# A causal mask moved out of the matrix engine's products, and a LoRA stage moved into the attention phase's tiles

## The chip, the core and the metric

The kernel runs on one core of a Trainium2 chip. A core has five engines with queues of their own: TensorE (PE, matrix products; PEld is its weight load), VectorE (DVE), ScalarE (ACT), GpSimd (POOL) and SyncE (SP, which here issues all DMAs). The metric is the device time of one execution in microseconds; lower is better. A profiled execution gives a page and a trace. L1391 means line 1391 of the kernel before.

## What is computed

Sixteen sequences of 512 tokens with 256 channels pass through six residual stages: a gated feed-forward with 4-bit block quantisation, a Mamba scan, the feed-forward again, a mixture of LoRA experts, causal attention with ALiBi, and the same mixture again. Each starts with a layer norm. The last three are what the change touches:

```python
x = x + 0.5 * lora(layernorm(x))
x = x + attn(layernorm(x))
x = x + 0.5 * lora(layernorm(x))

def lora(x):                            # 8 experts of rank 8
    result = x @ base_w.T + base_b
    gating = softmax(x @ router_w.T + router_b).astype(bfloat16)
    mid = x @ lora_A
    return result + 2 * einsum('bsr,erd,bse->bsd', mid, lora_B, gating)

def attn(x):                            # 16 heads of 16 channels
    q, k, v = heads(x @ Wq + bq), heads(x @ Wk + bk), heads(x @ Wv + bv)
    scores = q @ k.T / 4 - slope[h] * abs(kpos - qpos)
    scores = where(kpos > qpos, -inf, scores)
    return (softmax(scores) @ v) @ Wo + bo
```

## The kernel before

All sixteen sequences ("batches", b = 0 to 15) stay in SBUF as `xs[b]`, 128 partitions x 4 token blocks x 256. A framework (Tile) lays tiles into pools, puts in the waits, and orders each engine's instructions by priorities of its own, except where the kernel holds them to program order (`keep_in_program_order`): `matmul` (L1199) and `transpose` (L1202) of the attention phase do. A tile name with n buffers can be written for the (n+1)-th time only when its first use is done with.

**First LoRA stage**, `lora_phase` (L947), in pools of its own ("l" in SBUF; in PSUM two pools with the tags `ob`, `tr`, `o`, two buffers each, all eight banks). A software pipeline over b: `norm(b)` (statistics on DVE, a Sqrt on ACT, the reciprocal on DVE, four scalings on ACT), `turn(b-1)` (eight transposes, two copies on ACT), `base(b-2)` (sixteen matmul instructions as the trace counts them, with router and LoRA-A columns beside the 256; additions on DVE; a softmax over eight experts, whose Exp is on ACT) and `experts(b-3)` (transposes, a copy, eight matmuls, two additions). Sqrt and Exp are in different ACT tables, and each change costs an ACT_TABLE_LOAD. Between its steps the stage calls the generator `constants(aw)` (L1102), which loads attention's weights and fills its constant tiles. Behind the last batches it norms and turns batch 0 again (L1071 to L1080) and projects it to queries, keys and values by `heads` (L1251), with value tiles as spare room.

**Attention**, `attn_phase` (L1084). After the LoRA pools are closed, pools "a" (SBUF), `ps_s` (PSUM: `sp` two buffers and `sw` one, two banks each) and `ps` (tag `mm`, two single banks) are opened, the ACT table for Exp and Ln is loaded (L1467), and `begin(1)` (L1471) starts batch 1's norm. A unit is a batch and a group j of four heads; 64 units are pipelined over three turns of the main loop. In turn u there are six steps (three parts of the triangle x two pairs of heads). Each step has for unit A = u the peak scores (`peak_score`, products of 32 rows) and their maxima (`peak_max`: DVE adds a causal mask, then reduces); for unit C = u - 1 (or, in step 0, for Dn = u - 2) the same scores the other way round with the maximum taken off (`weigh_score`), and the exponential into `eT` (`weigh_exp`). Step 0 also has `peak_rows` (transposes of the maxima `mx`, and `qm`, queries with the maximum in a row) and `apply`, the weighted sums of Dn's values with `eT`. `aside` (L1483) fills each step with pieces of the next batch's projections (`project`, L1205), divisions and output projections.

A head takes 32 rows of `qs` and `ks`: 16 channels, row RS = 16 for the ALiBi term, row RM = 17 for the maximum; the other 14 are zero. Eight DMAs on SP per `q` or `k` half bring the 16 channel rows of each head to their places (L1288).

The causal mask of the exponentials is on PE: `weigh_exp` adds -1e30 in PSUM with two products of a bf16 identity `id16` and `mask_k`, 128 columns wide in parts 0 and 1, 256 in part 2, before ACT's Exp reads the bank.

**Last LoRA stage** (L1515 to L1692): the same computation in attention's pools as generators (`mix_norm`, `mix_turn`, `mix_base`, `mix_experts`). `mix_norm` has Ln and Exp on ACT, and two Newton steps and two more operations on POOL, ten of 4 elements. `mix_rest` orders them in rounds. Its working tiles (`parts`, L1519) are the `q`/`k` tiles of batch 14, free by then, and one `eT` tile. Two batches (`mix_first`) run beside attention's last batch, the other fourteen mostly behind it.

Of the kernel before, what the change touches and what calls it, by code (L numbers as in the profile page):

```python
# [36 lines left out]
def macaron_kernel(  # L37
# [83 lines left out]
    def transpose_seq(xh, dst, psum_pool, tag, order=lambda ins: ins):  # L121

        for k in range(KD):
            pt = psum_pool.tile([P, SEQ], F32, name="pt", tag=tag)
            for c in range(NC4):
                order(nc.tensor.transpose(  # L126
                    pt[:, c * P : (c + 1) * P], xh[:, c, k * P : (k + 1) * P], ident
                ))
            nc.scalar.copy(dst[:, k, :], pt)

# [50 lines left out]
    def ffn_phase(weights, src, dst, prepare=None, raws=(), keep=()):  # L181
        wgT, wuT, wdT = weights
        HF = DFF // 2
        with tc.tile_pool(name="f", bufs=2) as fp, tc.tile_pool(
# [90 lines left out]
            def make_h(b, pair, j):  # L275
# [3 lines left out]
                for half in range(2):  # L279
# [11 lines left out]
                    nc.scalar.activation(sl, g, AF.Silu)  # L291
# [655 lines left out]
    def lora_phase(weights, last, beside=None, heads=None):  # L947


        wx, lb, br = weights  # L950
        W = D + NE + NR
        with tc.tile_pool(name="l", bufs=2) as lp, tc.tile_pool(
            name="l_b", bufs=2, space=PSUM
        ) as ps_b, tc.tile_pool(name="l_ps", bufs=2, space=PSUM) as ps:
            xhs, xTs, copies = {}, {}, []

            cbs = []
            for i in range(3):
                cb = lp.tile([P, NC4, NX], F32, name=f"cb{i}", tag=f"cb{i}", bufs=1)
                nc.gpsimd.memset(cb[:, :, NE * NR :], 1.0)  # L960
                cbs.append(cb)

            def norm(b):

                x = xs[b]
                st = lp.tile([P, NC4, 6], F32, name="st", tag="st")
                mv = lp.tile([P, NC4, 2], F32, name="mv", tag="mv")
                for c in range(NC4):
                    nc.vector.bn_stats(out=st[:, c, :], in_=x[:, c, :])
                    nc.vector.bn_aggr(out=mv[:, c, :], in_=st[:, c, :])  # L970
                sd = lp.tile([P, NC4], F32, name="sd", tag="sd")
                nc.scalar.activation(sd, mv[:, :, 1], AF.Sqrt, bias=eps)
                rs = lp.tile([P, NC4], F32, name="rs", tag="rs")
                nc.vector.reciprocal(rs, sd)
                nm = lp.tile([P, NC4], F32, name="nm", tag="nm")
                nc.vector.scalar_tensor_tensor(
                    nm, mv[:, :, 0], -1.0, rs, op0=ALU.mult, op1=ALU.mult
                )
                xh = lp.tile([P, NC4, D], F32, name="xh", tag="xh")
                for c in range(NC4):  # L980
                    nc.scalar.activation(
                        xh[:, c, :], x[:, c, :], AF.Identity,
                        bias=nm[:, c : c + 1], scale=rs[:, c : c + 1],
                    )
                xhs[b] = xh

            def turn(b):
                xT = lp.tile([P, KD, SEQ], F32, name="xT", tag="xT")
                transpose_seq(xhs.pop(b), xT, ps, "tr")
                xTs[b] = xT  # L990

            def base(b):

                xT = xTs.pop(b)
                s = lp.tile([P, NC4, NE + NR], F32, name="s", tag="s")
                for half in range(2):
                    o = ps_b.tile([P, 2, SEQ], F32, name="ob", tag="ob")
                    for j in range(2):
                        c = 2 * half + j
                        for k in range(KD):  # L1000
                            nc.tensor.matmul(  # L1001
                                o[:, j, :W], lhsT=xT[:, k, c * P : (c + 1) * P],
                                rhs=wx[:, k, :], start=(k == 0), stop=(k == KD - 1),
                            )
                    nc.vector.tensor_tensor(
                        s[:, 2 * half : 2 * half + 2, :], o[:, :, D:W],
                        br.unsqueeze(1).to_broadcast([P, 2, NE + NR]), op=ALU.add,
                    )
                    xc = xs[b][:, 2 * half : 2 * half + 2, :]
                    nc.vector.tensor_tensor(xc, xc, o[:, :, :D], op=ALU.add)  # L1010
                lg, mid = s[:, :, :NE], s[:, :, NE:]
                mx = lp.tile([P, NC4], F32, name="mx", tag="mx")
                nc.vector.tensor_reduce(mx, lg, axis=AX.X, op=ALU.max)
                ex = lp.tile([P, NC4, NE], F32, name="ex", tag="ex")
                nc.vector.tensor_tensor(
                    ex, lg, mx.unsqueeze(2).to_broadcast([P, NC4, NE]), op=ALU.subtract
                )
                nc.scalar.activation(ex, ex, AF.Exp)
                nc.vector.tensor_reduce(mx, ex, axis=AX.X, op=ALU.add)
                nc.vector.reciprocal(mx, mx)  # L1020
                gt = lp.tile([P, NC4, NE], BF16, name="gt", tag="gt")
                nc.vector.tensor_tensor(
                    gt, ex, mx.unsqueeze(2).to_broadcast([P, NC4, NE]), op=ALU.mult
                )
                cb = cbs[b % 3]
                nc.vector.tensor_tensor(
                    cb[:, :, : NE * NR].rearrange("p c (e r) -> p c e r", e=NE),
                    gt.unsqueeze(3).to_broadcast([P, NC4, NE, NR]),
                    mid.unsqueeze(2).to_broadcast([P, NC4, NE, NR]), op=ALU.mult,
                )  # L1030

            def experts(b):
                cb = cbs[b % 3]
                pt = ps.tile([P, SEQ], F32, name="ct", tag="tr")
                for c in range(NC4):
                    nc.tensor.transpose(
                        pt[:NX, c * P : (c + 1) * P], cb[:, c, :], ident
                    )
                cT = lp.tile([NX, SEQ], F32, name="cT", tag="cT")
                copies.append(nc.scalar.copy(cT, pt[:NX, :]))  # L1040
                for half in range(2):
                    o = ps.tile([P, 2, D], F32, name="o", tag="o")
                    for j in range(2):
                        c = 2 * half + j
                        nc.tensor.matmul(  # L1045
                            o[:, j, :], lhsT=cT[:, c * P : (c + 1) * P], rhs=lb,
                            start=True, stop=True,
                        )
                    xc = xs[b][:, 2 * half : 2 * half + 2, :]
                    nc.vector.tensor_tensor(xc, xc, o, op=ALU.add)  # L1050
                if last:
                    store_x(b)

            for b in range(NB + 3):
                if 0 <= b - 3:
                    experts(b - 3)
                if 0 <= b - 2 < NB:
                    base(b - 2)
                if 0 <= b - 1 < NB:
                    turn(b - 1)  # L1060
                if b < NB:
                    norm(b)
                if heads is not None:
                    if 0 < b < NB:
                        next(beside, None)
                        if b % 2:
                            next(beside, None)
                    if b == NB - 1:
                        for _ in beside:
                            pass  # L1070
                    if b == NB:  # L1071
                        norm(0)
                    if b == NB + 1:
                        turn(0)
                        first = heads(0, xTs.pop(0), None, ps, "tr", nc.tensor.matmul)
                        for _ in range(4):
                            next(first)
                    if b == NB + 2:
                        for _ in first:
                            pass  # L1080
        return copies[-1]


    def attn_phase(weights):  # L1084
# [4 lines left out]

        RS, RM = HD, HD + 1  # L1090
        NJ = NH // 4
# [10 lines left out]
        def constants(aw):  # L1102
# [46 lines left out]
            for i in range(2):  # L1149
                for j in range(NJ):  # L1150
                    q = aw.tile([P, SEQ], F32, name=f"q{i}{j}")
                    nc.vector.tensor_scalar(
                        q, pos, 0.0, is_s, op0=ALU.mult, op1=ALU.add
                    )
                    qs.append(q)
                    k = aw.tile([P, SEQ], F32, name=f"k{i}{j}")
                    nc.vector.tensor_scalar(
                        k, pos, slope[:, j : j + 1], neg_m, op0=ALU.mult, op1=ALU.add
# [36 lines left out]
        def at(b, j):  # L1195
            return (b % 2) * NJ + j

# [665 lines left out]
```

## Time and profile before

| | us |
|---|---|
| three runs | 4329.03, 4329.45, 4329.85 |
| median | 4329.45 |
| profiled execution | 4323.53 |
| its span, first to last instruction | 4321.8 |

The page gives each engine's busy time over that span:

```profile
PE 3980.8 (92%) x18786; PEld 2179.5 (50%) x18786; DVE 3735.6 (86%) x4950; ACT 2315.4 (54%) x3478; POOL 1672.8 (39%) x1102
```

These are averages over six stages. By the windows of the trace the first feed-forward and the scan last to 2440 us, the second feed-forward to about 2990, the first LoRA stage to 3141, attention to about 4213, and the rest of the last LoRA stage to the end. The costliest groups of the LoRA and attention stages, by the page (line, engine, operation, output<-input, partitions x elements, count | busy us, mean ns of one | idle time of that engine just before, and what ended it):

```profile
L1397 ACT ACTIVATE eT<-s 128x768 f32<-128x768 f32 (+1 forms) x384 | 338.6, 882 | 481.0 <-PE s L1200 481.0
L1200 PE MATMUL s<-k,q 32*128 32x256 f32 (+3 forms) x2048 | 479.5, 477 | 5.4 <-DVE mx L1350 4.5
L1350 DVE TENSOR_REDUCE mx<-s 128x2 f32<-128x1024 f32 (+3 forms) x512 | 410.3, 823 | 12.4
L1200 PE MATMUL s<-qm,k 32*128 32x512 f32 (+3 forms) x2048 | 387.1, 473 | 8.9 <-ACT eT L1397 7.7
```

The matmuls of attention all have line 1200, that of the helper, so they are told apart by their tiles. An fp32 product shows as two matmuls. Products of 32 rows run side by side in the array, so their busy time is not a sum; starts and distances between starts are what to read.

### The profile page before, as it was taken

The page shows a single profiled execution, that of the slowest core. Times are in us where ns is not written, and L with a number is a line of the kernel's source. Part 1 is how long each engine was busy: PE and PEld are TensorE (multiplying, and loading weights), DVE is VectorE, ACT ScalarE, POOL GpSimd, SP SyncE. Part 2 cuts the span into 40 slices and gives each one's busy share as a digit, 9 for nine tenths or more (in the row PEclk, how much of TensorE's full clock was granted, in tenths as well). Part 3 has the DMA queues.
Part 4 walks back from the last instruction along what each step waited for, and adds up shares of the span by engine and source line. Part 5 has one row for each costly group of instructions (what it writes and reads, how often), then busy time and mean ns, then how long its engine had stood idle before and what let it go on. Part 6 is the DMA issues. An engine that isn't in the chain of part 4 may idle for free. (4 is left out here: it accounts for less than half of the span.)

```text
span 4321.8 us, 51496 instructions
## 1 busy us (share of the span) xinstructions
PE 3980.8 (92%) x18786; PEld 2179.5 (50%) x18786; DVE 3735.6 (86%) x4950; ACT 2315.4 (54%) x3478; POOL 1672.8 (39%) x1102
## 2 busy tenths in 40 slices
PE   6999977989888899888888799998999999999999
PEld 4666632333333333333333466666745555555557
DVE  9999838999999999999999899997678778878776
ACT  4444346676767677677666344434624444444434
POOL 3000027888888888888889400000000000000001
PEclk9999999999999999999999999999989999999999
DMA  4000024344444444444442300000010000000002
GB/s 151 15 15 20 15 109 129 119 137 128 127 132 133 141 142 142 142 142 141 142 139 82 114 1 1 1 1 16 2 24 16 18 19 16 18 20 14 20 11 69
DMA packets 120895, 305.16 MB, mean 71 GB/s; under 512 B 25329, under 2 KB 45362, under 8 KB 104002
## 3 DMA queue, kind: packets, MB, share of 16 engines
q1 hardware_dynamic: 120642, 301.88, 22.3%
q8 instruction: 148, 2.42, 0.2%
q14 instruction: 105, 0.86, 0.1%
HBM read 239.68 MB, written 45.35 MB: 66 GB/s over the span
## 5 line engine op out<-in xcount | busy, mean ns | idle before, releaser
L487 POOL TENSOR_TENSOR bx<-dtu,bc 128x1024 f32<-128x1024 f32 x512 | 1193.6, 2359 | 47.5 <-DVE h L883 47.3
L493 PE MATMUL y<-g,ident 128*128 128x512 f32 x2048 | 1007.3, 630 | 130.3 <-DVE g L490 130.1
L883 DVE TENSOR_TENSOR_SCAN h<-da,bx 128x1024 f32<-128x1024 f32 x384 | 879.7, 2291 | 85.4 <-ACT da L484 48.8
L484 ACT ACTIVATE da<-dt,a_neg 128x511 f32<-128x511 f32 x1024 | 703.0, 688 | 217.7 <-DVE hs L883 117.6
L493 PEld LDWEIGHTS y<-g,ident 128*128 128x128 f32 x2048 | 388.3, 198 | 710.0 <-issue 461.9
L1397 ACT ACTIVATE eT<-s 128x768 f32<-128x768 f32 (+1 forms) x384 | 338.6, 882 | 481.0 <-PE s L1200 481.0
L490 DVE TENSOR_TENSOR g<-h,bc 128x1024 f32<-128x1024 f32 x384 | 468.9, 1221 | 28.6 <-DVE h L883 1.4
L1200 PE MATMUL s<-k,q 32*128 32x256 f32 (+3 forms) x2048 | 479.5, 477 | 5.4 <-DVE mx L1350 4.5
L1350 DVE TENSOR_REDUCE mx<-s 128x2 f32<-128x1024 f32 (+3 forms) x512 | 410.3, 823 | 12.4
L1200 PE MATMUL s<-qm,k 32*128 32x512 f32 (+3 forms) x2048 | 387.1, 473 | 8.9 <-ACT eT L1397 7.7
L1600 POOL MEMSET k<- 128x4 f32 x2 | 0.2, 105 | 950.4 <-DVE ku L1282 946.9
L1346 DVE TENSOR_TENSOR s<-s,mask 128x256 f32<-128x256 f32 (+1 forms) x384 | 199.3, 519 | 194.1 <-PE s L1200 191.2
L487 POOL TENSOR_TENSOR g<-hs,bc 128x1024 f32<-128x1024 f32 x128 | 301.3, 2354 | 157.7 <-DVE hs L883 140.4
L291 ACT ACTIVATE sl<-g 128x352 f32<-128x352 f32 x256 | 118.1, 464 | 384.6 <-PE g L286 381.6
L1200 PEld LDWEIGHTS s<-k,q 32*128 32x128 f32 x2048 | 218.6, 186 | 164.1 <-DVE s L1346 80.5
L883 DVE TENSOR_TENSOR_SCAN hs<-da,bx 128x1024 f32<-128x1024 f32 x128 | 291.9, 2281 | 2.5 <-ACT da L484 2.5
L493 PE MATMUL p<-xT,w_in 128*128 128x512 f32 x500 | 242.2, 607 | 19.7 <-ACT xT L484 10.1
L484 ACT ACT_TABLE_LOAD x170 | 218.1, 1283 | 3.0
L960 POOL MEMSET cb<- 128x4 f32 x3 | 0.2, 104 | 561.4 <-PE o L331 561.4
L1200 PEld LDWEIGHTS s<-qm,k 32*128 32x128 f32 x2048 | 170.8, 186 | 58.7 <-ACT eT L1397 42.0
L516 POOL MEMSET xs<- 128x12 f32 x2 | 0.2, 110 | 512.7 <-DMA xd<-x 512.7
L286 PE MATMUL g<-wgT,xT 128*128 128x352 f32 x512 | 182.4, 466 | 0.0
(311 smaller groups left out, 6925.6 us busy)
## 6 DMA issues: line engine op xcount, KB each, us to landing
bc<-bd SPq DMA_DIRECT2D x128, 1024.0 KB, 6.6
xs<-xc SPq DMA_DIRECT2D x240, 256.0 KB, 4.7
xc<-xp SPq DMA_DIRECT2D x60, 256.0 KB, 2.0
x<-_attn_hidden_states_dram SPq DMA_DIRECT2D x16, 512.0 KB, 7.6
xd<-x SPq DMA_DIRECT2D x16, 512.0 KB, 2.6
xo<-xd SPq DMA_DIRECT2D x16, 512.0 KB, 3.6
xe<-xo SPq DMA_DIRECT2D x16, 512.0 KB, 2.6
x<-xe SPq DMA_DIRECT2D x16, 512.0 KB, 10.2
```

Of the source, the lines that this page charges most:

```text
L286: nc.tensor.matmul(dst, lhsT=xT[:, k, c * P : (c + 1) * P], rhs=w[:, k, f0 : f0 + HF], start=(k == 0), stop=(k == KD - 1),)
L291: nc.scalar.activation(sl, g, AF.Silu)
L484: return tc.keep_in_program_order(nc.scalar.activation(out, in_, func, **kw))
L487: tc.keep_in_program_order(nc.gpsimd.tensor_tensor(out, in0, in1, op=op))
L490: tc.keep_in_program_order(nc.vector.tensor_tensor(out, in0, in1, op=op))
L493: tc.keep_in_program_order(nc.tensor.matmul(out, **kw))
L516: nc.gpsimd.memset(t[:, :, : DCONV - 1], 0.0)
L883: tc.keep_in_program_order(nc.vector.tensor_tensor_scan(flat(h), flat(das[t % 2]), flat(bxs.pop(t)), 0.0, op0=ALU.mult, op1=ALU.add,))
L1200: tc.keep_in_program_order(nc.tensor.matmul(out, **kw))
L1346: nc.vector.tensor_tensor(own, own, const["mask"][:, :w].unsqueeze(1).to_broadcast([P, 2, w]), op=ALU.add)
L1350: nc.vector.tensor_reduce(mx[:, t, 2 * pair : 2 * pair + 2, RM], s[:, :, off : off + (t + 1) * P], axis=AX.X, op=ALU.max,)
L1397: const["exp"] = nc.scalar.activation(eT[:, 2 * pair : 2 * pair + 2, e0 : e0 + w], s[:, :, :w], AF.Exp)
```

## The change

**The mask of the exponentials.** `id16`, `mask_k` and the products are gone. The zero rows 18 to 29 of a head now stand for the twelve 32-key blocks (four token blocks c, i = 1 to 3): `ks` has a 1 there for the keys of its block, and `mx`, hence `qm`, has -1e30 there for the queries of block c before 32 i. The score product itself so masks every 32-key block that lies wholly ahead of a query. What remains, keys ahead of the query within one block of 32, is set to zero after Exp by an `affine_select` on POOL, in place in `eT`.

```diff
+        BLOCKS = [(c, i, RM + 3 * c + i) for c in range(NC4) for i in range(1, 4)]
...
+            last = ks[-1]
+            nc.vector.tensor_scalar(last, pos, 0.0, neg_m, op0=ALU.mult, op1=ALU.add)
+            for c, i, row in BLOCKS:
+                nc.vector.tensor_scalar(
+                    last[:, P * c + 32 * i : P * c + 32 * i + 32],
+                    prow.to_broadcast([P, 32]), float(row), neg_m,
+                    op0=ALU.is_equal, op1=ALU.add,
+                )
...
-                    nc.vector.tensor_scalar(
-                        k, pos, slope[:, j : j + 1], neg_m, op0=ALU.mult, op1=ALU.add
-                    )
+                    nc.vector.scalar_tensor_tensor(
+                        ks[i * NJ + j], pos, slope[:, j : j + 1], last,
+                        op0=ALU.mult, op1=ALU.add,
+                    )
...
                     nc.gpsimd.memset(mx, 0.0)
+                    for c, i, row in BLOCKS:
+                        nc.gpsimd.memset(mx[: 32 * i, c, :, row : row + 1], MASKED)
...
         def weigh_exp(b, j, part, pair, s, eT):
-            w = len(WEIGH[part]) * P
-            for i in range(2):
-                matmul(
-                    s[:, i, :w], lhsT=const["id16"],
-                    rhs=const["mask_k"].rearrange("p i e -> p (i e)")[:, :w],
-                    start=False, stop=True, skip_group_check=True,
-                )
             w = 512 if part == 0 else 384
             const["exp"] = nc.scalar.activation(
                 eT[:, 2 * pair : 2 * pair + 2, e0 : e0 + w], s[:, :, :w], AF.Exp
             )
+            n = len(WEIGH[part])
+            own = eT[:, 2 * pair : 2 * pair + 2, e0 : e0 + n * P]
+            nc.gpsimd.affine_select(
+                out=own, in_=own, compare_op=ALU.is_ge, fill=0.0, base=0,
+                pattern=[[0, 2], [0, n], [1, P]] if n > 1 else [[0, 2], [1, P]],
+                channel_multiplier=-1,
+            )
```

**The first LoRA stage.** `lora_phase` and `heads` are gone (`heads` is again the body of `project`). Attention's pools are opened straight after the feed-forward. `mix_rest` becomes `mix_rounds(first)`, run once with 0 for the first stage and once with 2 as before for the last. While `free` is empty, that is in the first stage, `parts` works in two `eT` tiles, nothing is stored, and each round also takes a step of `constants`; from round 16 on batch 0's `project` runs between its steps. The ACT table is loaded behind the feed-forward's last Silu. All three value tiles are filled with ones by `constants`.

```diff
-            behind = lora_phase(weights, False, constants(aw), heads)
...
-                with tc.issue_after(behind.ins):
+                with tc.issue_after(silu[-1].ins):
                     const["exp"] = nc.scalar.preload_act_table_set("natural_log_exp_and_others")
...
+                    for n in range(first + 1, NB + 4):
...
+                        if first + 2 <= n < NB:
+                            mix_norm(n)
+                        if not free:
+                            if n < NB:
+                                next(making, None)
+                            if n == NB:
+                                begin(0)
+                                normed = coming.pop(0)
+                            if n == NB + 1:
+                                coming[0] = normed
                         for of in (
                             turn, base, base, expert, turn, base, expert, base, expert
                         ):
...
+                making = constants(aw)
+                for _ in range(2):
+                    rows_of.append(ap.tile([P, 4, EW], F32, name="eT", tag="eT"))
+                mix_norm(0)
+                mix_norm(1)
+                for _ in mix_rounds(0):
+                    next(coming.get(0, none_left), None)
+                for _ in coming.pop(0):
+                    pass
+                started.clear()
+                begin(1)
```

In the built program the instructions of PE, DVE, ACT, POOL and SP stand in the same order in both kernels up to the end of the second feed-forward (but for the table load). From the first `qm` on, ACT's are the same, PE's differ by the 768 mask products and DVE's by a few swaps of small operations.

## The prediction

> **What bounds the kernel now.** I read the page's totals and slices first, then the windows by stage, then the timeline inside the stages that the diff touches. By slices, TensorE (PE) is the engine that is full in the last third of the span, where both LoRA stages and attention lie. The windows divide that third (columns: start and end, length, then PE, PEld, DVE, ACT and POOL busy with instruction counts, granted clock, DMA share, GB/s).
>
> ```profile
> PE   6999977989888899888888799998999999999999
> DVE  9999838999999999999999899997678778878776
> POOL 3000027888888888888889400000000000000001
> 2990.00:3141.00 151.00, 132.66 (x634) 102.84 (x633) 106.58 (x415) 94.49 (x174) 3.78 (x12) 0.97 0.06 15
> 3141.00:3175.00 34.00, 27.58 (x81) 11.06 (x82) 23.76 (x67) 3.99 (x8) 2.11 (x2) 0.60 0.14 31
> 3175.00:4110.00 935.00, 927.28 (x7650) 499.08 (x7649) 739.97 (x1371) 391.19 (x520) 0.10 (x1) 0.99 0.08 18
> ```
>
> Three stages, three limits. The first LoRA stage (2990 to 3141) has PE at 88%, DVE at 71%, ACT at 63%. The first attention unit (3141 to 3175) runs at a granted clock of 0.60. Attention proper has PE busy 99% of 935 us, DVE 79%, POOL nothing: a microsecond taken out of PE's stream there is a microsecond of span, as long as DVE can follow. All earlier stages issue the same instructions in both kernels, and so do ACT and (but for a few small swaps) DVE in attention: they are costed at nothing because nothing of them changes.
>
> **Part 1: the mask products leave PE.** Each of the 384 exponentials (64 units of 4 heads, 6 each) is preceded by two bf16 products of `id16` with `mask_k` (L1391): 128 columns in parts 0 and 1, 256 in part 2. Their busy time overlaps their neighbours', so I take the distance from the first product of a pair to the next other matmul:
>
> ```profile
> 3601.05 0.39 PE L1200 MATMUL s<-mask_k,id 128*128 128x256 bf16 x2
> 3601.37 1.12 PE L1200 MATMUL s<-k,q 32*128 32x512 f32 x2
> ...
> 3607.82 0.28 PE L1200 MATMUL s<-mask_k,id 128*128 128x128 bf16 x2
> 3607.94 0.61 PE L1203 MATMUL p<-ident,oT 128*128 128x128 f32 x4
> ```
>
> 0.12 us for a narrow pair, 0.32 for this wide one (0.23 where a transpose follows). Summed so over the trace: 256 narrow pairs 35.3 us, 128 wide pairs 37.7, together 73.0, or 1.14 per unit. A unit takes 16.05 us (from one `qm` to the next, over a batch: 17.7, 15.3, 15.6, 15.6), so PE alone would bring it to 14.9.
>
> Not all of that is had. DVE is busy 13.4, 13.5, 12.8 and 11.3 us in those four units; the second would have 13.5 in 14.1. And at a quarter of the unit borders the transposes of `mx` already wait 0.35 us for DVE's last maximum, where 0.23 of mask is hidden anyway: 16 x 0.23 = 3.7. I give back 12 us in all, 4 for those borders and 8 (half a microsecond per batch) for the tight unit. Bounds: 0 back, or half of the gain (36) if DVE's order becomes the limit.
>
> **Part 2: GpSimd's selection stands between exp and the weighted sum.** POOL gets 384 selections on fp32, in place: 256 elements a partition (parts 0, 1) or 512 (part 2). Only the last of a unit can be felt: the next PE work after it is that unit's `apply`, whose third block (c = 2) reads what it wrote. The rows:
>
> ```profile
> L1177 POOL TENSOR_SCALAR_AFFINE_SELECT mask_k<-mask_k x2: 292/292/292, 3031.5 to 3031.7; 128x128 bf16<-128x128 bf16 x2
> 3603.40 0.39 PE L1200 MATMUL s<-mask_k,id 128*128 128x256 bf16 x2
> 3603.83 0.81 ACT L1397 ACTIVATE eT<-s 128x768 f32<-128x768 f32 x1 [1.54 <-PE s L1200]
> 3604.45 2.36 PE L1200 MATMUL o<-eT,va 128*32 128x512 f32 x32
> ```
>
> Take M as the moment when the scores end and the mask pair now starts. In most units exp ends at M + 1.24 and c = 2 starts 1.05 later, at M + 2.29. Without the pair PE's c = 2 comes 0.23 earlier, at M + 2.06; exp needs no mask and, with the same distance from last matmul to exp (0.3 us), ends at about M + 0.95. ACT to POOL costs 0.08 (ACT `rs` ending 4201.20, POOL `g` starting 4201.28), POOL to the next about the same. So the selection has some 0.95 us. The trace has it only at 128 elements. Below, a POOL memset of 512 (0.52 us); above, four times 0.292 (1.17; the 1024-element product at 2.36 us gives the same rate). Splitting 0.292 into the 0.104 of a 4-element memset and a rest that grows with the elements, 0.104 + 4 x 0.188 = 0.86: just hidden. I charge 3 us; bounds 0 and 64 x 0.25 = 16. POOL has the room: 4 x 0.48 + 2 x 0.86 = 3.6 us of a 15 us unit, with nothing else queued there but the 10-op norm chains of the last batch.
>
> The Trainium skill ("GPSIMD Engine Reference", 3.1) has about 1.8 cycles per element at 1.2 GHz at best for a one-input loop; 512 elements would be 0.77 us before dispatch, by an estimate from that page, and the charge would be 0. The same skill speaks against the change in "SBUF — State Buffer" (SBUF: two separate sides): a DVE instruction with two SBUF inputs and a reading GpSimd instruction exclude each other for their whole length. The row it bears on is `x<-x,bob` (682 ns, two a batch); if every one of the 32 held up a last selection it would be 32 x 0.68 = 22 us. But the one that stands nearest to a unit's border, at 3601.46, starts 2.3 us before that unit's last exp does, so by this rule only stray ones could count, under 2 us. No run here shows the lock.
>
> **Part 3: the first LoRA stage in the rounds of the last one.** Removed are the Sqrt and Exp table loads, 9 of each at 1.28 us; the norm becomes Ln and Exp on ACT (0.2 us each) and ten 4-element POOL operations, 2.7 us a batch (4201.28 to 4204.02).
>
> ```profile
> 3013.83 0.60 PE L126 MATMUL pt<-ident,xh 128*128 128x128 f32 x4
> ...
> 3118.10 1.04 PE L126 MATMUL pt<-ident,xh 128*128 128x128 f32 x8
> ...
> 4263.69 0.20 ACT L1545 ACTIVATE rs<-v 128x4 f32<-128x4 f32 x1
> ...
> 4270.40 0.21 ACT L1545 ACTIVATE rs<-v 128x4 f32<-128x4 f32 x1
> ```
>
> From the third batch's transposes to the sixteenth's the old stage takes 104.3 us, 8.0 a batch. The last stage, which has the rounds already, repeats every 6.7 with PE never waiting. The first one also carries the statistics (4 x 0.41 + 4 x 0.16 a batch) and the constants on DVE, so I take 7.2: 13 x 0.8 = 10.5 gained; bounds 17 and 0.
>
> Its start: POOL now does five large memsets (2 x 0.52, 3 x 1.06), 24 small ones (0.04 to 0.10 each) and two iotas before the first norm chain, 6 to 7.5 us from 2993.9, then 2.7 of chain. First transposes at 3003 to 3005 instead of 2999.9. DVE's next `mv` waits for POOL there, with base(0)'s additions queued behind it. Batches 2 and 3 share one chain, and I get the third batch's transposes at 3014, as now: 0, within 3 either way.
>
> Its end: after the last transposes there remain 5.8 us of that round, base(15) 3.6, three `mix_experts` at 2.1 (lag 4, not 3) and the projections 11.2, some 27, plus 3 of waits in two shared PSUM banks: 30 against 22.9 now (3118.1 to 3141.0). 7 lost; bounds 4 and 12. The stage: 4 gained, from 13 gained to 12 lost. The 32 q/k row DMAs (0.62 us each on SP) are the same ones in the same order, and begin before the last three expert steps as now.
>
> **Part 4: the first unit.** Norm 1 now uses a pool that opened long before:
>
> ```profile
> 3148.55 2.30 PE L1203 MATMUL p<-ident,xh 128*128 128x128 f32 x8 [6.42 <-DVE xh L1235]
> 3157.94 1.65 PE L1200 MATMUL s<-k,q 32*128 32x256 f32 x8
> ```
>
> Today PE starts at 3141.0, idles 6.4 us because `xh` of batch 1 was begun only then, and runs on at half clock; the first `qm` comes at 3168.3, 27.3 us later. In the new order that `xh` stands on DVE before the last softmaxes of the LoRA stage. Then the unit is DVE's six additions and maxima, 2 x 1.65 + 2 x 1.38 + 2 x 1.72 = 9.5, plus 2.5 for first score, transposes and waits: 12. Gain 15; bounds 16 and, if the clock falls again, 3.
>
> **Sum.** -73 + 12 + 3 - 15 - 4 = -77. The span of 4321.8 becomes 4245, its execution (1.7 more) 4246.5. The three runs' median, 4329.45, is 5.9 above the profiled execution; on it I put the same difference: 4252.
>
> **The rivals.** (a) DVE becomes the bound in attention and half of part 1 is lost: -36 + 3 - 15 - 4 = -52, 4277. For it: 13.5 us of 14.1 in the tight unit. Against: 51 us of 59.6 over a batch, two score buffers. (b) The LoRA stage comes out 12 longer (POOL's memsets first, two PSUM banks) and PE is cold again in unit 0: -73 + 12 + 3 - 3 + 12 = -49, 4280. For it: the queue order above; against: the last stage's 6.7. (c) Slower: the selection itself. It costs 64 times what it exceeds 0.95 us by, and eats the remaining 80 at 0.95 + 80/64 = 2.2 us for 512 elements, 4.3 ns each, nearly twice the 2.3 of any row. At 3 us: 64 x 2.05 = 131, 4380. (d) No change: the pairs were hidden by drains of the array that stay; then parts 1 and 2 give nothing and part 3 loses what part 4 wins, 4329. Against: PE's next work follows each pair at once.
>
> **How the numbers follow.** Forecast 0.70 (4232 to 4270), (a) 0.14, (b) 0.08, (c) 0.05, (d) 0.03. A change of 0.2%, some 9 us, is about what can be told from none: faster 0.92, same 0.03, slower 0.05. The range reaches from all parts near their better bounds to (b) with a little over: 4228 to 4286.
>
> **What would show it.** Right: units of about 15.1 us from `qm` to `qm`; no `mask_k`; the last selection near 0.86 us and `o` waiting little for POOL; the first LoRA stage at 7.2 us a batch; the first `qm` some 12 us after the first score. Wrong: `o` waiting for POOL over 0.3 us a unit, PE waiting for `mx` all over attention, a clock of 0.6 again behind the LoRA stage.

## The result and the profile after

The changed kernel takes 4265.14 us (median of 4 runs, 4263.2 to 4267.94) against 4329.62 for the kernel before: a ratio of 0.9855, 95% interval 0.9841 to 0.987, or 64 us less. Forecast were 4252 and 77 us less; the time lies in the range given, and the gain is 13 us short of the likeliest case. The time also lies midway between the likeliest case and the 4277 of rival (a). The profiled execution took 4263.2 with a span of 4261.5; it lies 1.9 us under its median and the profiled execution of before 5.9 under its own, so the two profiles differ by 60 us and not by 64.

The page's totals and slices of after (engine, busy us, share, instructions; then tenths of 40 slices):

```profile
PE 3906.4 (92%) x18018; PEld 2131.2 (50%) x18018; DVE 3739.3 (88%) x4954; ACT 2293.5 (54%) x3473; POOL 1900.3 (45%) x1669
...
PE   6999987988899988888898799999899999999989
...
POOL 3000027888889888888988600000401111111121
```

PE has 768 products fewer and 74 us less busy time; POOL, empty in attention before, now shows a tenth to two. Busy time fell by what was forecast, the span by less: so the question is what PE's stream did with the room. The windows by stage of after (start and end, length, then PE, PEld, DVE, ACT, POOL busy, granted clock, DMA share, GB/s):

```profile
2991.00:3131.00 140.00, 125.76 (x624) 100.50 (x625) 117.07 (x463) 69.62 (x168) 42.85 (x197) 0.94 0.07 19
3131.00:3143.50 12.50, 11.52 (x57) 5.16 (x58) 11.56 (x19) 1.76 (x3) 0.00 (x0) 1.00 0.15 35
3143.50:3210.00 66.50, 61.48 (x436) 30.43 (x439) 50.30 (x93) 25.56 (x33) 11.62 (x24) 0.87 0.08 18
3210.00:4050.00 840.00, 816.47 (x6526) 428.64 (x6519) 691.67 (x1278) 367.27 (x488) 160.40 (x326) 1.00 0.08 18
```

The first unit's 27 us at a clock of 0.60 are 12.5 us at 1.00. In attention proper PE was 99% busy before and is 97% now: about 1 us in a unit of two of every four is idle, so something other than PE sets those units.

The landmarks of the new first LoRA stage in PE's timeline: transposes of the third and the sixteenth batch, the first score, and the transposes of batch 1, which no longer wait for their `xh`:

```profile
3012.79 0.60 PE L1077 MATMUL p<-ident,xh 128*128 128x128 f32 x4
...
3100.64 0.60 PE L1077 MATMUL p<-ident,xT 128*128 128x128 f32 x4
...
3130.87 1.14 PE L1074 MATMUL s<-k,q 32*128 32x512 f32 x8
3131.95 1.09 PE L1077 MATMUL p<-ident,xh 128*128 128x128 f32 x8
```

The times between landmarks of the two profiled executions, in us:

| stretch | before | after | difference | forecast |
|---|---|---|---|---|
| start to the last product of the second feed-forward | 2993.8 | 2991.4 | -2.3 | 0 |
| from there to the first attention score | 147.2 | 139.4 | -7.8 | -4 |
| first score to first `qm` | 27.3 | 12.5 | -14.8 | -15 |
| first to last `qm` (63 units) | 1020.9 | 987.7 | -33.2 | -58 with the next row |
| last `qm` to the end | 132.6 | 130.4 | -2.2 | |
| span | 4321.8 | 4261.5 | -60.3 | -77 |

The first row is no effect of the change (the same instructions in the same order; in the traces of all ten kernels this end lies within 5 us); the shortfall is all in attention. There a steady batch takes 61.7 us (units of 17.0, 14.7, 14.9 and 15.1) instead of 64.1. The pairs' distances in such a batch of before sum to 4.20 us; it got 2.44. (The 73.0 of the whole trace would be 4.56 a batch on average, but outside the steady batches three distances, of 1.04, 1.54 and 2.30 us, hold waits of PE for DVE's maxima. These are the products behind those three pairs, with the idle time before them in brackets.)

```profile
3193.82 0.48 PE L1200 MATMUL s<-k,q 32*128 32x256 f32 x1 [0.76 <-DVE mx L1350]
3196.35 0.79 PE L1200 MATMUL s<-k,q 32*128 32x256 f32 x1 [1.25 <-DVE mx L1350]
4139.89 0.55 PE L1203 MATMUL p<-ident,mx 128*128 128x128 f32 x3 [1.91 <-DVE mx L1350]
```

**Where the 1.8 us a batch went.** I laid the two traces of one batch beside each other, product group by product group, and read where the distance between the same groups shrinks and where it grows again. It shrinks at each removed pair, grows by 0.05 to 0.10 at nearly every group that follows one, shrinks again at most of the score groups behind those, and grows by more at two of the four unit borders. First the small steps. The same place in the two timelines, PE and its weight loads (start, us, then operation; "x2" are two instructions in one line), before:

```profile
3583.28 0.38 PE L1200 MATMUL s<-k,q 32*128 32x128 f32 x2
3583.59 0.11 PEld L1200 LDWEIGHTS <-id 128*128 128x128 bf16 x2
3583.60 0.28 PE L1200 MATMUL s<-mask_k,id 128*128 128x128 bf16 x2
3583.66 0.30 PEld L1200 LDWEIGHTS p<-xT,wk 128*128 128x128 f32 x2
3583.72 1.08 PE L1200 MATMUL p<-xT,wk 128*128 128x512 f32 x2
3584.73 0.48 PE L1200 MATMUL s<-k,q 32*128 32x256 f32 x1
```

and after:

```profile
3545.30 0.38 PE L1074 MATMUL s<-k,q 32*128 32x128 f32 x2
3545.60 0.30 PEld L1074 LDWEIGHTS p<-xT,wk 128*128 128x128 f32 x2
3545.61 1.12 PE L1074 MATMUL p<-xT,wk 128*128 128x512 f32 x2
3546.66 0.48 PE L1074 MATMUL s<-k,q 32*128 32x256 f32 x1
```

Before, the weights of `p<-xT,wk` are loaded 0.06 us ahead of the product, while the second mask product still streams. After, load and product start together, and the two products reach the next scores 1.05 us later instead of 1.01. The pair had hidden part of the next load. There are 342 places where a group of 128-row products follows a pair. Behind a narrow pair (233 places) the distance from the first to the second product is 0.05 us longer after: 0.115 became 0.165 for transposes, 0.272 became 0.320 for 256 columns, 0.485 became 0.533 for 512. Behind a wide one it is 0.10 longer (46 places: 0.218 became 0.320, 0.432 became 0.533), or 0.055 where the transposes of `mx` follow (63). That is 1.20 us in a steady batch.

Most of it comes back one group later. The score products `s<-qm,k` behind many pairs wait until an Exp has read the bank that they write, and without the mask that Exp begins earlier. Before:

```profile
3561.24 0.60 PE L1200 MATMUL s<-qm,k 32*128 32x512 f32 x2
3561.78 0.28 PE L1200 MATMUL s<-mask_k,id 128*128 128x128 bf16 x2
3561.90 1.08 PE L1200 MATMUL p<-xT,wq 128*128 128x512 f32 x2
3562.10 1.02 ACT L1397 ACTIVATE eT<-s 128x1024 f32<-128x1024 f32 x1 [1.51 <-PE s L1200]
3563.18 0.58 PE L1200 MATMUL s<-qm,k 32*128 32x384 f32 x1
```

and after:

```profile
3523.89 0.60 PE L1074 MATMUL s<-qm,k 32*128 32x512 f32 x2
3524.42 1.12 PE L1074 MATMUL p<-xT,wq 128*128 128x512 f32 x2
3524.58 1.02 ACT L1245 ACTIVATE eT<-s 128x1024 f32<-128x1024 f32 x1 [1.37 <-PE s L1074]
3525.65 0.58 PE L1074 MATMUL s<-qm,k 32*128 32x384 f32 x1
```

In both, the last row starts 0.05 us behind the end of the Exp. From the first row to the last it is 1.94 us before and 1.76 after: 0.17 gained (unrounded), where the pair's distance is 0.12 and the first product is 0.05 slower. At 15 of the 24 places of this batch of before the next such product starts 0.05 us behind an Exp's end like this. In all, 0.91 of the 1.20 comes back, so the hidden loads cost 0.29 us a batch net, 4.6 over sixteen.

Then the two borders, where a batch loses 0.61 us (ahead of the second unit) and 0.85 (the fourth unit's). The steps of a steady batch so add up: 4.20 - 1.20 + 0.91 - 0.61 - 0.85 = 2.45. At the first of the two, DVE's timeline in after, and POOL's:

```profile
3533.65 1.70 DVE L1109 TENSOR_SCALAR xh<-x,mv,rs 128x256 f32<-128x256 f32 x4
3535.27 0.42 DVE L1201 TENSOR_TENSOR s<-s,mask 128x256 f32<-128x256 f32 x1
3535.61 0.23 DVE L1089 BATCH_NORM_AGGREGATE mv<-st 128x2 f32<-128x6 f32 x2
3535.76 1.19 DVE L1205 TENSOR_REDUCE mx<-s 128x2 f32<-128x1024 f32 x1
3536.87 0.67 DVE L1221 TENSOR_TENSOR qm<-q,p 128x512 f32<-128x512 f32 x1
```

```profile
3531.25 0.64 POOL L1251 TENSOR_SCALAR_AFFINE_SELECT eT<-eT 128x512 f32<-128x512 f32 x1 [1.47 <-ACT eT L1245]
3534.36 0.84 POOL L1251 TENSOR_SCALAR_AFFINE_SELECT eT<-eT 128x512 f32<-128x512 f32 x1 [2.48 <-ACT eT L1245]
```

DVE runs without a gap from 3530 on: the four scalings `xh` of a later batch's norm stand ahead of the mask and the last maximum, and `qm`, on which PE waits, ends the row. This is the "tight unit" of the prediction. New in it is the 1.70: the same four take 1.38 before. The last one takes 0.72 instead of 0.41 where a selection runs beside it, and that selection takes 0.84 instead of the usual 0.64. All xh scalings of the trace, and the selections (min, median and max in ns):

```profile
L1109 DVE TENSOR_SCALAR xh<-x,mv,rs x64: 403/409/728, 3097.3 to 3968.0; 128x256 f32<-128x256 f32 x64
```

```profile
L1251 POOL TENSOR_SCALAR_AFFINE_SELECT eT<-eT x384: 406/408/842, 3146.5 to 4152.5; 128x256 f32<-128x256 f32 x128, 128x512 f32<-128x512 f32 x64
```

A selection of 256 elements takes 0.41 us, one of 512 takes 0.64 (the forecast had 0.48 and 0.86). Nothing else of DVE's that recurs shows a longer time beside a selection in after: `x<-x,bob`, which the prediction named, keeps its 0.68 in 14 overlaps of 0.17 us. At the other late border, the fourth unit's, the transposes of `mx` wait for the last maximum. The waits of PE in attention proper, from 3175 to 4110 (engine and line that waits, what for, us in all, times, longest):

```profile
PE p L1077 <- DVE mx L1205: 13.6, 16, 2.2
PE s L1074 <- ACT eT L1245: 8.4, 16, 0.5
PE s L1074 <- DVE qm L1221: 6.3, 14, 1.2
```

Before, the first of these rows and the last are not there: both borders, some 20 us, are DVE's. POOL is not in PE's list. It is in that of the weight loads, which run ahead of the products:

```profile
PEld o L1074 <- POOL eT L1251: 11.4, 44, 0.7
```

Whether these waits of loads delay a product is what `no_select` below settles.

### The profile page after: what moved, and what is told of

The parts are those of the page before. It is cut to its first block, busy times and chain, and to the rows that moved or that the text cites. A ratio compares the mean times of both kernels' runs of the same rounds, so it can differ in the third digit from the quotient of the medians.

```text
span 4261.5 us, 50531 instructions
## 1 busy us (share of the span) xinstructions
PE 3906.4 (92%) x18018; PEld 2131.2 (50%) x18018; DVE 3739.3 (88%) x4954; ACT 2293.5 (54%) x3473; POOL 1900.3 (45%) x1669
## 5 line engine op out<-in xcount | busy, mean ns | idle before, releaser
L1251 POOL TENSOR_SCALAR_AFFINE_SELECT eT<-eT 128x256 f32<-128x256 f32 (+1 forms) x384 | 189.4, 493 | 863.6 <-ACT eT L1245 863.6
L1074 PE MATMUL s<-k,q 32*128 32x256 f32 (+3 forms) x2048 | 459.6, 470 | 9.0 <-DVE mx L1205 5.8
L1205 DVE TENSOR_REDUCE mx<-s 128x2 f32<-128x1024 f32 (+3 forms) x512 | 410.0, 822 | 12.5
L1074 PEld LDWEIGHTS s<-k,q 32*128 32x128 f32 x2048 | 206.4, 185 | 171.1 <-issue 94.0
```

Of the source, the lines that this page charges most:

```text
L1074: tc.keep_in_program_order(nc.tensor.matmul(out, **kw))
L1205: nc.vector.tensor_reduce(mx[:, t, 2 * pair : 2 * pair + 2, RM], s[:, :, off : off + (t + 1) * P], axis=AX.X, op=ALU.max,)
L1251: nc.gpsimd.affine_select(out=own, in_=own, compare_op=ALU.is_ge, fill=0.0, base=0, pattern=[[0, 2], [0, n], [1, P]] if n > 1 else [[0, 2] ...
```

## The experiments

Eight kernels, in two sessions on the chip, each beside runs of the kernel before, whose medians there were 4326.4 and 4326.0 us. So ratios are compared: after's is 0.9855, and 0.001 is 4.3 us.

### mask_only and lora_only: the two halves of the change

On the kernel before, only the mask's change:

```diff
+        BLOCKS = [
+            (c, i, RM + 3 * c + i) for c in range(NC4) for i in range(1, 4)
+        ]
...
+            last = ks[-1]
...
+                    for c, i, row in BLOCKS:
+                        nc.gpsimd.memset(mx[: 32 * i, c, :, row : row + 1], MASKED)
...
-                matmul(
-                    s[:, i, :w], lhsT=const["id16"],
-                    rhs=const["mask_k"].rearrange("p i e -> p (i e)")[:, :w],
...
+            nc.gpsimd.affine_select(
+                out=own, in_=own, compare_op=ALU.is_ge, fill=0.0, base=0,
```

> The mask change alone, on the kernel before with its old first LoRA stage. Theory: in the trace of after the steady units give 2.44 us a batch from qm to qm, 33 us over the 63 intervals and 2 behind them, so about 4329.5 - 36 = 4294, with units of 15.4 us and the 27 us start of attention at half clock kept. Rival (the prediction's sizes, -73 + 12 + 3 = -58 for parts 1 and 2, and the loss elsewhere): 4271. Second rival (the two parts of the change depend on each other and the mask needs the new stage): clearly above 4300.

Measured: 4293.49 us, ratio 0.9925 (0.9912 to 0.9939), 33 us less. Units of 17.0, 14.7, 14.9 and 15.1 as in after, the first `qm` 27.2 us behind the first score, and the first products of a group at 0.165, 0.320 and 0.534. The theory's 36 us less, which was read from the trace of after, lies in the interval; the 58 of the prediction's sizes does not.

The other half is after with the inverse of these lines: `id16`, `mask_k` and the 768 products back, no spare rows, no selection.

> The moved LoRA stage alone: after with the mask products back on PE, no spare rows, no selection. Theory: 7.8 us from the stage and 14.8 from the first unit, 4329.5 - 23 = 4307 (prediction's sizes: -19, 4310); units of 16.05 us again, first products behind the mask pairs at 0.115 (transposes) and 0.485 us (512 columns) instead of the 0.165 and 0.533 of after. Rival (the new stage also changes attention's units): a unit period other than 16.05 and a time under 4300 or over 4315.

Measured: 4302.74, ratio 0.9943 (0.9931 to 0.9956), 24 us less. Units of 17.7, 15.3, 15.6 and 15.6, as before; first products back at 0.116, 0.272 and 0.484; first `qm` 12.5 us behind the first score. So the new stage does not touch attention's units. The halves make 33 + 24 = 57 us, the whole 63; the difference is inside the intervals (some 6 us each). The longer first products come and go with the pairs, in each kernel with and without them.

### no_select: what the selection costs

```diff
-            nc.gpsimd.affine_select(
-                out=own, in_=own, compare_op=ALU.is_ge, fill=0.0, base=0,
-                pattern=[[0, 2], [0, n], [1, P]] if n > 1 else [[0, 2], [1, P]],
-                channel_multiplier=-1,
-            )
```

> After without the 384 selections, so keys ahead of the query within one block of 32 are not masked. Theory: the selection is no main loss. It slows one xh scaling a batch from 0.41 to 0.72 us ahead of the tight border (14 x 0.3 = 4) and is waited for 47 times by PE's loads, a tenth of a microsecond or so each: 5 to 8 us less than after's 4265, so 4257 to 4260. Rival (the selection is what holds back the missing 20 us of attention): 4245.

Measured: 4257.59, ratio 0.9841 (0.9827 to 0.9854): 6 us less than after by the ratios, whose intervals overlap. The trace decides. Laid beside after, a steady batch differs at one place only, the border shown above, by 0.31 us; all other groups stand at the same distances to 0.01. DVE's scalings there and over the whole trace of no_select:

```profile
3529.96 1.38 DVE L1109 TENSOR_SCALAR xh<-x,mv,rs 128x256 f32<-128x256 f32 x4
```

```profile
L1109 DVE TENSOR_SCALAR xh<-x,mv,rs x64: 405/408/416, 3096.9 to 3960.4; 128x256 f32<-128x256 f32 x64
```

So in a steady batch the selection costs nothing by its own latency, and 0.31 us through the scaling that it slows: 13 x 0.31 = 4.0 us in all. It is not what holds back the missing gain.

### half_mask: is DVE the limit at those borders?

```diff
-            nc.vector.tensor_tensor(
-                own, own, const["mask"][:, :w].unsqueeze(1).to_broadcast([P, 2, w]), op=ALU.add
-            )
+            if j == 0:
+                nc.vector.tensor_tensor(
+                    own, own, const["mask"][:, :w].unsqueeze(1).to_broadcast([P, 2, w]), op=ALU.add
+                )
```

> After without DVE's causal mask ahead of the maxima in the groups of heads j = 1 to 3 (the maximum there also covers later keys of the query's own token block, which only shifts the exponent). It takes some 2.5 us of DVE out of three units of four. Theory: two borders a batch are DVE's (the second unit's, 0.7 us short of its pairs, and the fourth's, 0.4), and DVE's relief gives these back: 1.0 x 15, about 4250, with the first products behind score groups still at 0.165 and 0.533. Rival (what is missing went all into the slower first products and DVE is not waited for): 4265, no change from after.

Measured: 4246.46, ratio 0.9814 (0.9801 to 0.9827), some 18 us less than after. Beside after, a steady batch is shorter at exactly two places: 0.47 us at the second unit's border and 0.85 at the fourth's, 1.32 in all (units of 17.0, 14.1, 14.9, 14.4). The window of attention proper, to be held against after's:

```profile
3210.00:4050.00 840.00, 829.33 (x6671) 436.57 (x6670) 591.80 (x1058) 373.64 (x499) 163.38 (x350) 1.00 0.08 19
```

With 100 us less of DVE, PE is busy 829 instead of 816 us of the 840 and gets some 145 more products through. The first products stay at 0.165, 0.320 and 0.534. So DVE's borders are the larger cause (of their 1.32 us some 0.35 were there before the change, as the prediction read): with DVE relieved a steady batch gets 3.77 of the pairs' 4.20 us, where after gets 2.44. Of the 0.43 still missing 0.14 is at the second unit's border, and 0.29 is the net of the weight loads, which no relief of DVE touches. The version keeps the result, since a larger number taken off all exponents of a row cancels in the division. How much larger it gets is bounded by the slopes: at most 127 x 0.177 = 22 in the exponent by the position term for j = 1 to 3, but 127 x 0.71 = 90 for j = 0, which is why those heads keep the mask.

### double_select: how much room the selection had

```diff
-            nc.gpsimd.affine_select(
...
+            for _ in range(2):
+                nc.gpsimd.affine_select(
```

> After with each selection made twice in place (the second changes nothing). In after the last selection of a unit takes 0.64 us and the weighted sum's third block starts 0.32 us behind its end in some 32 units of 64, 0.11 in 13, over 0.9 in 18. Theory (a selection costs what it exceeds that margin by): a second 0.64 is felt with 0.64 - 0.27 = 0.37 in the 32 and with 0.58 in the 13, 12 + 8 = 20 us, and the second selection can meet more of the xh scalings, up to 4: after's 4265 + 20 to 24, about 4287. Rival (POOL runs far enough beside and what was lost to the selection was the slowed xh only): 4265 to 4270. Rival (the selection delays every unit in proportion): 64 x 0.64 = 41, 4306.

Measured: 4303.33, ratio 0.9948 (0.9934 to 0.9963), 40 us more than after. That is the number of the proportional rival, but the trace shows the theory's waits: beside after, the weighted sums of three units of a steady batch end 0.45 us later, those of the fourth do not, and the tight border loses another 0.37 to slowed scalings. 3 x 0.45 + 0.37 = 1.7 us a batch, or 26 us over fifteen. The rest is the clock: between the fifth and the last `qm` the trace has twelve stretches at half clock, 41.0 us, where after has four, 13.7; half of the 27.3 between them is 14 us. The window:

```profile
3210.00:4050.00 840.00, 812.01 (x6257) 418.80 (x6256) 677.71 (x1237) 351.73 (x468) 302.66 (x626) 0.98 0.08 18
```

The second selection starts 0.71 us behind the first, and 0.45 of it is felt: the single one had 0.26 us to spare. "Just hidden" was right, with more room than the 0.09 forecast.

### late_fill and half_late: POOL's memsets at the stage's start

```diff
-                        nc.gpsimd.tensor_scalar(g, g, -1.0, None, op0=ALU.mult)
+                        const["normed"] = nc.gpsimd.tensor_scalar(g, g, -1.0, None, op0=ALU.mult)
...
+            with tc.issue_after(const["normed"].ins):
...
                    nc.gpsimd.memset(mx, 0.0)
```

> After with POOL's five large and 24 small memsets held behind a later norm chain instead of ahead of the first. Theory (the prediction's step: the memsets delay the first norms): in after the first transposes come 10.6 us behind the second feed-forward's last product, before 6.8; without the memsets about 7.5, so 3 us less, 4262, and less time at half clock. Rival (the chain of ten POOL operations and the wait for the weights set the start): 4265, first transposes again 10 us behind.

Measured: 4263.64, ratio 0.9858 (0.9841 to 0.9874): no change. The step itself is there. The first transposes of after and of late_fill, with the idle time of PE ahead of them in brackets:

```profile
3001.43 1.95 PE L1077 MATMUL p<-ident,xh 128*128 128x128 f32 x4 [9.98 <-DVE prow L999]
```

```profile
2998.95 2.38 PE L1078 MATMUL p<-ident,xh 128*128 128x128 f32 x6 [7.52 <-ACT xh L1427]
```

The first score comes 2.4 us earlier against the feed-forward's end, and the profiled execution loses as much in attention's first four units (67.7 instead of 66.6 us) and at unit 60 (18.1 instead of 16.8). In both, stretches at half clock fall differently; why was not tried. `half_late` is half_mask with this edit:

> Both: DVE's mask only in the groups j = 0, and the late memsets. Theory: the two lie in different stages and add, half_mask's ratio 0.9814 and 3 us: 0.9807 of before. Rival (the gain at the start is taken back by the clock or by a later wait): 0.9814.

Measured: 4243.09, ratio 0.9808 (0.9793 to 0.9823). The theory's number, though half_mask's 0.9814 lies in the interval as well: a gain of 3 us cannot be told from none here. With 83 us less than before it is the fastest kernel of this study.

### half_late_b2: the norm moved off the border

```diff
-                    if A and A[1] == 2 and A[0] + 2 < NB:
-                        begin(A[0] + 2)
...
+                        if n == 2 and A and A[1] == 2 and A[0] + 2 < NB:
+                            begin(A[0] + 2)
```

> half_late, with the next norm begun in the third step of the unit instead of ahead of its first, so that DVE has the four xh scalings behind qm and not ahead of it. Theory: in half_mask qm of every fourth unit still comes 0.5 us late because xh (0.41 x 3 and 0.78 beside a selection) stands ahead of the last maximum; moved, that border gives 0.5 x 14 = 7 us: 0.9790 of before. Rival (the scalings then hold up the maxima in mid-unit, and PE waits for a score buffer there): 0.9807 or more.

Measured: 4248.61, ratio 0.9821 (0.9807 to 0.9836): no gain. The unit of 17.0 did fall to 15.1, but the next rose from 14.1 to 16.6, the third from 14.9 to 14.7: 60.9 a batch against 60.4. DVE's 4 us of norm are as much in the way inside the next unit as at its border: in the window 3210 to 4050 PE waits 13 times, 5.2 us in all, with transposes and 13 times, 2.1 us, with scores for DVE's maxima, and in `half_late` not at all. The rival holds.

## Why the prediction came out as it did

**Part 1, the pairs.** The order of the removed work and its place on PE's path were right, and so was that PE follows at once. Wrong was the size: "Summed so over the trace: 256 narrow pairs 35.3 us, 128 wide pairs 37.7, together 73.0". The distances of a steady batch sum to 4.20 us, 67 over sixteen; the rest of the sum is mostly waits for DVE's maxima, 0.76, 1.25 and 1.91 us, at three places outside them. And the distance from a pair to the next product is not what its removal gives: where PE's own stream sets the pace a narrow pair of 0.12 gave 0.08, because it hid part of the next weight load; where the next scores wait for an Exp it gave 0.11 to 0.20. Net the loads cost 0.29 a batch. Rows of before could have warned: there every load of a 128-row product behind a narrow pair starts 0.05 us ahead of its product, most behind a wide pair 0.11.

**What is given back.** Forecast were 12 us at borders and 3 for the selection, 0.94 a batch. The two borders were the ones named, but a steady batch gives back 1.46, 19 us over the thirteen steady batches; half_mask, by relieving DVE, gets 1.32 of it back. By border: the tight one 0.61 where 0.69 was forecast (8 + 3 us over sixteen), the fourth unit's 0.85 where 0.25 was. So the fourth unit's border is the term that was mis-sized. Inside the tight one the selection's share is 0.31 (no_select), by another way than the one priced: not its own latency, but the scaling that takes longer beside it.

For that way the prediction had weighed another instruction. The Trainium skill ("SBUF — State Buffer", SBUF: two separate sides) names two kinds of DVE instruction that shut GpSimd out and are shut out by it: those with two SBUF inputs and those in a two-port performance mode. I weighed `x<-x,bob`, of the first kind, in which the trace of after shows no loss (0.68 in 14 overlaps of 0.17 us); double_select has one, overlapped for 0.36 us, that took 0.91. What did meet the selection is `xh`, one input and two scalars, 0.72 us instead of 0.41 in 13 of 14 batches (0.78 in half_mask), which would agree with the second kind; that it runs in that mode no trace says, and no run tells a shared port from another cause. It stood in the trace of before, 2.9 to 1.5 us ahead of `qm` at the tight border.

**Part 2's timing.** 0.64 us instead of 0.86 for 512 elements, 0.26 to spare instead of 0.09; doubled, the selection is waited for. The rate of the Trainium skill's page ("GPSIMD Engine Reference", 3.1), by which the prediction had estimated 0.77 for 512, lies above what was measured too.

**Part 3, the stage.** Forecast 7.2 us a batch; from the third batch's transposes (3012.8) to the sixteenth's (3100.6) it is 87.9 us, 6.76 each, as in the last stage. The statistics and constants on DVE were no limit, 16.4 us gained instead of 10.5. The end behind the last transposes took 30.2 (forecast 30). The start cost 1.3 against the feed-forward's end where I had 0, first transposes at 3001.4. Sum -7.8 instead of -4.

**Part 4, the first unit.** 12.5 us and no half clock, forecast 12: as written.

**What no step had.** Between first and last `qm` the trace of after has 30.7 us at half clock, before had 17.6. Half of the difference, by this estimate 6.6 us, is lost; why was not tried. Two of these stretches lie in steady batches, 1.7 us each. So the 33.2 us of that row are 13 x 2.44 = 31.7 less 3.4 in the steady batches, 1.4 in the four units ahead of them and 3.3 in the seven behind, 33.0.

**Together.** Parts 1 and 2 were forecast at 58 us, 3.6 a batch, and a steady batch got 2.4. Of the missing 1.2, some 0.36 is the sum of distances (4.56 instead of 4.20), 0.29 the loads, and 0.52 DVE's borders (1.46 instead of 0.94). The parts on the stage and the first unit gave 3.6 us more than forecast. That the total came within 13 us of the forecast is in part luck: errors of both signs stand in the sum.

Of the rivals, (a) has the mechanism of the two borders but not their size: DVE held back 19 us in the steady batches, not 36. (b) is refuted by the stage's 6.76 and the clock of 1.00 behind it, (c) by the 0.26 us to spare, (d) by the units.

## What to carry to other kernels

The time from an instruction's start to the next one's start is not yet what its removal gives. Look at what was being prepared under it (here a weight load that began 0.05 to 0.11 us ahead of the product behind the pair), and at who releases the group behind that: where it waits for another engine that the removal lets begin earlier, the gain can be larger than the distance (0.17 for 0.12). And before such distances are summed, look at those that stand out: three of 384 held 3.9 us of waits. Before an idle engine is given work, list which instructions of the neighbour engine run at that moment on the late path, all kinds of them, and not only the one that a rule brings to mind. And when PE's stream gets shorter, the engine that was second becomes the bound at single borders long before its mean load says so: DVE at 82% cost 1.3 us a batch, and taking operations off it gave 18 us more, where moving them within the batch gave none.

## What was not expected of the hardware

The half-clock stretches in attention do not simply follow PE's idle time: in the window 3210 to 4050 PE is idle 5.1 us before, 23.5 in after, 19.5 in no_select, 10.7 in half_mask and 28.0 in double_select, and the trace has 1, 4, 2, 4 and 12 such stretches between the fifth and the last `qm`, of mostly 3.4 us. A stretch makes its unit 1.7 us longer (16.8 instead of 15.1 in after's). What starts one was not tried, so part of any microsecond that PE is made to wait may come back larger, as in double_select, where 26 us of waits cost 40.

A selection and a scaling `xh` that meet seem to take turns: in half_mask the selection that starts first keeps its 0.64 and `xh` takes 0.78; in after, where the third scaling is under way, the selection takes 0.84 and the fourth scaling 0.72.
